# Edge scores of a four-layer graph network: units stationary, one column of signs streamed, scores with slots on partitions

## The chip, the cores and the metric

The kernel runs on one core of one Trainium2 chip. The metric is device time in microseconds (us): the median of several executions of the whole kernel. The engines are PE (TensorE, matrix products; its weight loads are listed apart as PEld), DVE (VectorE), ACT (ScalarE), POOL (GpSimd) and SP (which issues DMAs).

## The reference

Sixteen graphs of 1024 nodes with 128 features go through four layers. Layers 0, 1 and 3 work on the dense 1024x1024 adjacency matrix. The change concerns layer 2 alone, which runs two rounds (`L` = 2) of this:

```python
for l in range(L):
    a = jnp.einsum('bnd,de->bne', x, We1[l, :D])
    b = jnp.einsum('bnd,de->bne', x, We1[l, D:])
    h = jax.nn.relu(a[:, :, None, :] + b[:, None, :, :] + be1[l])
    scores = jax.nn.sigmoid(jnp.squeeze(h @ We2[l], -1) + be2[l])
    upd_adj = adjacency * scores
    messages = jnp.einsum('bnm,bmd->bnd', upd_adj, x)
    ...     # update of x from [x, messages]
```

A pair of nodes with a zero in the adjacency matrix needs no score. About 1.6% of the pairs have an edge, so the kernel before computes the scores of edges only.

## The kernel before

**Buckets and slots.** The 1024 nodes are 8 tiles of 128. A bucket is a pair of tiles (t, u) with t <= u, and holds its edges, undirected, in slots: at most 320 in one of the 28 buckets off the diagonal (`C_OFF`), 480 in one of the 8 diagonal ones (`C_DIAG`). Slots are taken in chunks of 128 (`CK_OFF` = 3, `CK_DIAG` = 4). For each batch `build` makes 0/1 matrices in fp8 for every bucket: `on` and `om` say which node is at either end of a slot (nodes on partitions, slots along the row), and `onT` and `omT` are the same with slots on partitions. `turned` makes such a transposition by matrix products with an identity (tiles `pn`, `pm`). The last chunk of a bucket off the diagonal is half full (`TAIL` = 64); its 64 slots are held twice, in both halves of the partitions, so that the high and the low half of a score can use one product.

**Groups.** Four buckets form a group; a round has seven groups off the diagonal (in which each bucket is done in both directions, so eight rows of scores) and two diagonal ones (four rows). There are 16 x 2 = 32 rounds, hence 224 groups off the diagonal and 64 diagonal ones. For a group:

1. `gather` (L1028): four products bring the parts of both ends to the slots: `pre`, features on partitions, 320 or 480 slots along the row.
2. L1045 (ACT) and L1046 (DVE) apply the relu and split the result in two fp16 halves: `hid`, high and low.
3. `dots` (L1062), as soon as four `hid` are there: the weights We2 were folded into the earlier products with only their signs left, so the score is a sum over features with signs. A 128x32 block of `slide` (zeros but for one column of signs) is stationary, and each half of each `hid` streams through it. The four `hid` write to four 32-partition quarters of one PSUM bank `sc`. Eight products to a call, two calls to a group off the diagonal, one to a diagonal group: 4096 products in the run. A score row lies along the row of one partition.
4. `ends` (L1083, ACT): tanh of the whole `sc` to `srow`. Off the diagonal in two instructions, since the last 64 slots are written twice.
5. `scores`, called while the next group is gathered: transposes of `srow` (L1095, 3 or 4 chunks, fp32) to `pt`, in the same PSUM bank as `sc`; then the columns in use are split in two fp16 halves `u` (L1100 ACT, L1101 DVE, and off the diagonal the small copy L1107); then `val` = `onT` or `omT` times the score (L1120, DVE).
6. `scatter` (L1145): products of `omT`/`onT` with `val` make score matrices `p`; L1153 multiplies by the adjacency; `messages` (L195) multiplies by the features.

**Order.** Every engine works through its own list in order. `weave` mixes three generators by written-down costs: `main` (layer 2 of batch b), `first` (layers 0 and 1 of batch b+1 and its `build`) and `last` (layer 3 of batch b-1). The change leaves these costs alone. PSUM has eight banks: two for `pre`, one each for the lanes `a` and `c`, two for the message sums, one for `sc` (shared with `pt`) and one for `p`.

Of the kernel before, what the change touches and what calls it, by code (L numbers as in the profile page):

```python
# [9 lines left out]
F32 = mybir.dt.float32  # L10
F16 = mybir.dt.float16
FP8 = mybir.dt.float8e4
I32 = mybir.dt.int32
AF = mybir.ActivationFunctionType
OP = mybir.AluOpType
# [36 lines left out]
def tile_four_gnn_layers(  # L52
# [409 lines left out]
    def slots(t, s):  # L462

        return (C_DIAG, CK_DIAG) if t == s else (C_OFF, CK_OFF)

    class Batch:


# [72 lines left out]
    class Edges:  # L541
# [31 lines left out]
        def constants(self):  # L573
            con = self.con
            self.eye16 = con.tile([P, P], F16, name="eye16")
            nc.vector.tensor_copy(self.eye16, ident)
            self.ones16 = con.tile([P, 1], F16, name="ones16")
            nc.vector.memset(self.ones16, 1.0)
            self.iota2 = con.tile([P, HALF], F16, name="iota2")
            self.tri2 = con.tile([P, P], F16, name="tri2")  # L580
            self.low2 = con.tile([P, P], F16, name="low2")
            odd = con.tile([P, CK_DIAG], F32, name="odd")
            i0 = self.a.scratch("i0").bitcast(I32)[:, :Q]
            nc.gpsimd.iota(i0, pattern=[[2, HALF]], base=0, channel_multiplier=0)
            nc.vector.tensor_copy(self.iota2, i0)
            i1 = self.a.scratch("i1").bitcast(I32)[:, 0]
            nc.gpsimd.iota(i1, pattern=[[1, P]], base=0, channel_multiplier=-1)

            nc.vector.tensor_scalar(self.low2, i1, 0.0, 2.0, op0=OP.is_gt, op1=OP.mult)
            nc.vector.tensor_add(self.tri2, self.low2, ident)  # L590
            i2 = self.a.scratch("i2").bitcast(I32)[:, 0, :CK_DIAG]
            nc.gpsimd.iota(i2, pattern=[[2 * P, CK_DIAG]], base=1, channel_multiplier=2)
            nc.vector.tensor_copy(odd, i2)

            iota_off = con.tile([P, CK_OFF * P], F16, name="iota_off")
            nc.vector.tensor_copy(iota_off[:, :C_OFF], self.iota2[:, :C_OFF])
            nc.vector.tensor_copy(iota_off[:, C_OFF:], self.iota2[:, C_OFF - TAIL : C_OFF])
            odd_off = con.tile([P, CK_OFF], F32, name="odd_off")
            nc.vector.tensor_copy(odd_off, odd[:, :CK_OFF])
            last = odd_off[TAIL:, CK_OFF - 1 : CK_OFF]  # L600
            nc.vector.tensor_scalar(last, last, -2.0 * TAIL, None, op0=OP.add)
            self.iota = {True: self.iota2, False: iota_off}
            self.odd = {True: odd, False: odd_off}
            self.c.fine = con.tile([P, 1], F32, name="fine")
            nc.vector.memset(self.c.fine, 1.0)

            self.srow = con.tile([P, CK_DIAG * P], F32, name="srow")
            nc.vector.memset(self.srow, 0.0)

            self.most = con.tile([P, 2], F32, name="most")  # L610
            nc.vector.memset(self.most, 0.0)

        def scaled(self):
# [10 lines left out]
            nc.tensor.matmul(ps, w3T, a3_sb, start=True, stop=True)  # L624
            nc.vector.tensor_copy(v3, ps)
            spread_v3(0)
            self.slide = con.tile([P, L, 2 * G - 1], F16, name="slide16")
            nc.vector.tensor_copy(self.slide, slide)

            self.be2 = con.tile([P, L], F32, name="be2_s")  # L630
            nc.vector.tensor_scalar(self.be2, be2_bc, 0.5, None, op0=OP.mult)
# [193 lines left out]
        def rows_hot(self, s, t, u, name):  # L825

            ck, i = slots(t, u)[1], INDEX[t, u]
            far = self.work.tile([P, HALF], F16, tag="far", name=f"far_{name}")
            nc.scalar.activation(
                far[:, : ck * P], self.iota[t == u][:, : ck * P], AF.Abs, bias=s.mid[:, i : i + 1]  # L830
            )
            on = self.hot_tile("on", t, u, ck * P, name)
            nc.vector.tensor_scalar(
                on, far[:, : ck * P], s.wid[:, i : i + 1], None, op0=OP.is_le, saturate=False
            )
            return on

        def turned(self, hot, ck, name):

            ps = self.a.one(name)  # L840
            for k in range(ck):
                nc.tensor.matmul(  # L842
                    ps[:, k * P : (k + 1) * P], hot[:, k * P : (k + 1) * P], self.eye16,
                    start=True, stop=True,
                )
            return ps

        def build(self, s, has, name):
# [5 lines left out]
            for g, grp in enumerate(GROUPS):  # L854
# [13 lines left out]
                for i, (t, u) in enumerate(grp):  # L868
# [13 lines left out]
                    nc.scalar.activation(onT, pn[:, : ck * P], AF.Copy, saturate=False)  # L882
                    yield 0.35
                    pq = self.a.one(f"pq_{nm}").rearrange("p (k m) -> p k m", m=P)
                    for k in range(ck):
                        nc.tensor.matmul(  # L886
                            pq[:, k], on[:, k * P : (k + 1) * P], rank[:, i], start=True, stop=True
                        )
                    nc.vector.tensor_tensor(  # L889
                        omT.rearrange("p (k m) -> p k m", m=P), pq[:, :ck],  # L890
# [1 line left out]
                        op=OP.is_equal, saturate=False,  # L892
                    )
                    yield 0.35
                    pm = self.turned(omT, ck, f"pm_{nm}")
                    om = self.hot_tile("om", t, u, c, nm)
                    nc.scalar.activation(om, pm[:, :c], AF.Copy, saturate=False)  # L897
                    s.on[t, u], s.om[t, u] = on, om
# [77 lines left out]
        class Group:  # L976
# [3 lines left out]
            def __init__(self, path, s, l, k, msg, name):  # L980
# [3 lines left out]
                self.c, self.ck = slots(*self.grp[0])  # L984
                self.nd = 1 if self.diag else 2
                self.rows = self.nd * Q
                self.per = self.rows // J
                self.hid, self.done, self.sc = [], 0, None

                self.runs = []  # L990
                for i, (t, u) in enumerate(self.grp):
# [60 lines left out]
            def dots(self):  # L1052

                if self.sc is None:
                    self.sc = self.path.bank("sc", f"sc_{self.name}")
                while len(self.hid) - self.done >= J:
                    r = self.done // J

                    order = [(1, J - 1)] + [(0, g) for g in range(J)] + [(1, g) for g in range(J - 1)]
                    with ExitStack() as behind:  # L1060
                        for n, (v, g) in enumerate(order):
                            ins = nc.tensor.matmul(  # L1062
                                self.sc[g * G : (g + 1) * G, : self.c],
                                self.path.slide[:, self.l, G - 1 - r : 2 * G - 1 - r],
                                self.hid[self.done + g][:, v, : self.c],
                                start=(r == 0 and (v, g) in order[: J]),
                                stop=(r == self.per - 1 and (v, g) in order[J:]),
                            )
                            if n == 0:
                                behind.enter_context(tc.issue_after(ins.ins))  # L1070
                    self.done += J

            def ends(self):

                row, once = self.path.srow, self.c if self.diag else self.c - TAIL
                parts = [(row[:, :once], self.sc[:, :once])]
                if not self.diag:
                    parts.append((
                        row[:, once : self.ck * P].rearrange("p (i n) -> p i n", i=2),
                        self.sc[:, None, once : self.c].to_broadcast([P, 2, TAIL]),  # L1080
                    ))
                for dst, src in parts:
                    nc.scalar.activation(  # L1083
                        dst, src, AF.Tanh, bias=self.path.be2[:, self.l : self.l + 1],
                        scale=self.path.down[:, self.l : self.l + 1],
                    )

            def scores(self):


                path, ck, per, name = self.path, self.ck, self.per, self.name
                row = path.srow
                pt = path.bank("sc", f"pt_{name}")
                for k in range(ck):
                    nc.tensor.transpose(pt[:, k * P : (k + 1) * P], row[:, k * P : (k + 1) * P], ident)  # L1095
                pt = pt[:, : ck * P].rearrange("p (c r) -> p c r", r=G)[:, :, :per]
                u = path.work.tile([P, CK_DIAG * J * 2], F32, tag="u", name=f"u_{name}")
                u = u[:, : ck * J * per]
                u2 = u.bitcast(F16).rearrange("p (c r h) -> p c r h", r=per, h=2)
                nc.scalar.activation(u2[:, :, :, 1], pt, AF.Copy, scale=S_SCALE)  # L1100
                nc.vector.scalar_tensor_tensor(  # L1101
                    u2[:, :, :, 0], pt, S_SCALE, u2[:, :, :, 1], op0=OP.mult, op1=OP.subtract
                )
                if not self.diag:

                    again = u2[TAIL:, (ck - 1) * J :]
                    nc.vector.tensor_copy(again[:, :, :, 1], again[:, :, :, 0])  # L1107
                u = u.rearrange("p (k g r) -> p k g r", g=J, r=per)
                self.val, self.ps = {}, [None] * self.nd

                nd = self.nd
                for d in range(nd):
                    for i in range(0, Q, 2):
# [2 lines left out]
                        )  # L1116
                        right = self.s.pairs[self.grp[i]]["omT" if d else "onT"]
                        j = i * nd + d
                        v = u[:, :, j % J : j % J + nd + 1 : nd, j // J : j // J + 1]
                        nc.vector.tensor_tensor(  # L1120
                            pair[:, :, :ck], right, v.rearrange("p k i o -> p i k o").to_broadcast(
                                [P, 2, ck, P]
# [346 lines left out]
```

## Time and profile before

| | |
|---|---|
| median of three runs | 5272.19 us (5258.7 to 5277.03) |
| profiled execution, span | 5272.1 us |
| granted PE clock, mean | 0.986 |
| PE busy | 4924.4 us, 44997 products |
| DVE busy | 4225.4 us |
| ACT busy | 3069.1 us |
| `dots` products (L1062) | 4096, busy 222.2 + 44.4 us |
| transposes of score rows (L1095) | 928, busy 156.2 us |
| tanh of score rows (L1083) | 512, busy 126.1 + 101.7 + 48.0 us |

The span of the profiled execution is the median within 0.1 us, so nothing has to be added around it. Busy time of PE counts a product from its start to its modelled end, and neighbours overlap: three products of 128 columns in a row take 0.33 us, of which only the first 0.055 us each is time that the next can't use. The start of one product to the start of the next is therefore what a product costs.

### The profile page before, as it was taken

How to read it: one execution, taken by the hardware profiler on the slowest of the kernel's cores; microseconds unless marked ns; L12 is line 12 of the kernel's file. 1: busy time of each engine (PE TensorE's matmuls, PEld its weight loads, DVE VectorE, ACT ScalarE, POOL GpSimd, SP SyncE). 2: the span in 40 equal slices, each digit the busy share in tenths (PEclk: the TensorE clock that was granted, in tenths of full speed). 3: DMA queues.
4: the chain of work that ended last, by engine and by line, in shares of the span. 5: the costliest groups of instructions: out<-in, count | busy, mean ns of one | idle time of the engine just before them, and what ended most of it. 6: DMA issues, size and time to landing. Idle time of an engine off the chain costs nothing.

```text
span 5272.1 us, 112168 instructions
## 1 busy us (share of the span) xinstructions
PE 4924.4 (93%) x44997; PEld 3714.9 (70%) x44997; DVE 4225.4 (80%) x9542; ACT 3069.1 (58%) x6790; POOL 199.2 (4%) x137
## 2 busy tenths in 40 slices
PE   6999999999999999999999999999999999999986
PEld 5776777777776777777777776777777777777664
DVE  4776787878879788797887879788797887978876
ACT  5555574665647556575665747556475565756533
POOL 0000000000000000000000000000000000000000
PEclk8999999999999999999999999999999999999998
DMA  6243425243252433424243252432424334242121
GB/s 187 83 127 97 119 59 152 83 132 106 80 155 65 137 98 102 136 66 140 89 123 114 64 165 68 140 100 86 143 75 129 97 102 135 66 139 87 54 64 48
DMA packets 740129, 554.46 MB, mean 105 GB/s; under 512 B 32273, under 2 KB 686353, under 8 KB 739601
## 3 DMA queue, kind: packets, MB, share of 16 engines
q1 hardware_dynamic: 734496, 545.58, 34.8%
q8 instruction: 355, 5.82, 0.5%
q10 hardware_dynamic: 5104, 1.65, 0.1%
q14 instruction: 174, 1.42, 0.1%
HBM read 446.44 MB, written 100.66 MB: 104 GB/s over the span
## 4 chain that ended last, share of the span: by engine, by line
PE 52%; DVE 23%; ACT 13%; DMA 7%; POOL 2%; issue 2%; SPq 0%; ACTq 0%; POOLq 0%; DVEq 0%
PE pre L1028 13%; DVE val L1120 6%; PE p L1145 6%; PE nb L301 6%; PE msg L195 4%; DMA at<-in_adj_dram 4%; PE sc L1062 3%; PE h L355 3%; DVE hid L1046 3%; PE bb L309 3%; PE hp L195 3%; DMA a<-adjT 2%; PE pq L886 2%; ACT hid L1045 2%; PE pn L842 2%
## 5 line engine op out<-in xcount | busy, mean ns | idle before, releaser
L1045 ACT ACTIVATE hid<-pre 128x320 f16<-128x320 f32 (+1 forms) x2048 | 914.6, 453 | 648.3 <-PE pre L1028 597.9
L1046 DVE SCALAR_TENSOR_TENSOR hid<-pre,hid 128x320 f16<-128x320 f32 (+1 forms) x2048 | 1011.8, 506 | 291.3 <-ACT hid L1045 269.6
L1028 PEld LDWEIGHTS <-part 128*128 128x128 f16 x8192 | 749.2, 98 | 410.7 <-issue 179.8
L1028 PE MATMUL pre<-on,part 128*128 128x320 fp8e4 (+1 forms) x4096 | 976.2, 308 | 22.2 <-DVE hid L1046 18.2
L1028 PE MATMUL pre<-om,part 128*128 128x320 fp8e4 (+1 forms) x4096 | 967.0, 308 | 0.0
L195 PE MATMUL msg<-upd,xf 128*128 128x128 f32 (+3 forms) x3008 | 605.4, 321 | 0.7 <-DVE upd L1153 0.6
L1120 DVE TENSOR_TENSOR val<-onT,u 128x768 f32<-128x768 fp8e4 (+1 forms) x576 | 561.1, 1010 | 2.6
L1145 PE MATMUL p<-val,omT 128*128 128x128 f16 x6528 | 498.1, 219 | 50.5 <-DVE val L1120 43.3
L1145 PEld LDWEIGHTS <-omT 128*128 128x128 fp8e4 x6528 | 419.4, 96 | 91.7 <-issue 47.1
L195 PEld LDWEIGHTS msg<-upd,xf 128*128 128x128 f32 x3008 | 418.6, 192 | 20.9 <-DVE upd L1153 2.3
L897 ACT ACTIVATE om<-pm 128x320 fp8e4<-128x320 f32 (+1 forms) x576 | 268.6, 466 | 250.7 <-PE pm L842 247.6
L1120 DVE TENSOR_TENSOR val<-omT,u 128x768 f32<-128x768 fp8e4 x448 | 410.8, 950 | 0.0
L1153 DVE SCALAR_TENSOR_TENSOR upd<-p,adj 128x512 f32<-128x512 f32 x512 | 349.2, 682 | 52.6 <-PE p L1145 48.9
L1145 PE MATMUL p<-val,onT 128*128 128x128 f16 x4480 | 368.2, 219 | 2.4 <-DVE upd L1153 2.4
L195 PE MATMUL hp<-wh,e 128*128 128x129 f32 x2048 | 334.9, 285 | 14.5 <-DVE e L515 14.3
L882 ACT ACTIVATE onT<-pn 128x384 fp8e4<-128x384 f32 (+1 forms) x576 | 297.5, 516 | 83.1 <-PE pn L842 79.3
L1145 PEld LDWEIGHTS <-onT 128*128 128x128 fp8e4 x4480 | 298.6, 97 | 36.1 <-issue 9.9
L1083 ACT ACTIVATE srow<-sc,be_s,down 128x128 f32<-128x128 f32 (+2 forms) x512 | 255.7, 539 | 109.7 <-PE sc L1062 107.8
L195 PEld LDWEIGHTS hp<-wh,e 128*128 128x128 f32 x2048 | 282.1, 195 | 36.4 <-issue 15.0
L301 PE MATMUL nb<-z,l 128*128 128x128 f32 x2048 | 270.8, 282 | 26.2 <-DVE o L342 26.2
L301 PEld LDWEIGHTS nb<-z,l 128*128 128x128 f32 x2048 | 252.9, 196 | 58.5 <-DVE o L342 32.7
L889 DVE TENSOR_TENSOR omT<-pq,odd_off 128x384 fp8e4<-128x384 f32 x448 | 247.5, 552 | 47.3 <-PE pq L886 41.4
(213 smaller groups left out, 8073.3 us busy)
## 6 DMA issues: line engine op xcount, KB each, us to landing
at<-in_adj_dram SPq DMA_DIRECT2D x128, 512.0 KB, 4.0
ct<-in_adj_dram SPq DMA_DIRECT2D x128, 512.0 KB, 4.6
adjT<-tn SPq DMA_DIRECT2D x128, 512.0 KB, 4.8
l<-adjT SPq DMA_DIRECT2D x128, 512.0 KB, 4.4
adj<-adjT SPq DMA_DIRECT2D x256, 256.0 KB, 3.5
a<-adjT SPq DMA_DIRECT2D x128, 384.0 KB, 3.4
adj<-adjT SPq DMA_DIRECT2D x448, 64.0 KB, 2.1
adj<-adjT SPq DMA_DIRECT2D x192, 128.0 KB, 2.6
```

Source lines behind the costliest of these rows:

```text
L195: ins = nc.tensor.matmul(dst, left, right, start=opened is None, stop=True, skip_group_check=True)
L301: nc.tensor.matmul(ps, mat[:, k], z[:, k], start=(k == 0), stop=(k == T - 1))
L882: nc.scalar.activation(onT, pn[:, : ck * P], AF.Copy, saturate=False)
L889: nc.vector.tensor_tensor(omT.rearrange("p (k m) -> p k m", m=P), pq[:, :ck], self.odd[t == u][:, :, None].to_broadcast([P, ck, P]), op=OP ...
L897: nc.scalar.activation(om, pm[:, :c], AF.Copy, saturate=False)
L1028: ins = nc.tensor.matmul(pre[:, :c], path.parts[node // Q][:, k, node % Q, v], hot[:, :c], start=(hot is on and k == 0), stop=(hot is om a ...
L1045: nc.scalar.activation(hid[:, 0, :c], pre[:, :c], AF.Relu)
L1046: nc.vector.scalar_tensor_tensor(hid[:, 1, :c], pre[:, :c], 0.0, hid[:, 0, :c], op0=OP.max, op1=OP.subtract)
L1083: nc.scalar.activation(dst, src, AF.Tanh, bias=self.path.be2[:, self.l : self.l + 1], scale=self.path.down[:, self.l : self.l + 1],)
L1120: nc.vector.tensor_tensor(pair[:, :, :ck], right, v.rearrange("p k i o -> p i k o").to_broadcast([P, 2, ck, P]), op=OP.mult,)
L1145: nc.tensor.matmul(self.ps[d][:, i], left[:, k], halves[:, k, :, h], start=(k, h) == terms[0], stop=(k, h) == terms[-1],)
L1153: nc.vector.scalar_tensor_tensor(upd, self.ps[d], S_SCALE, self.adj[:, d * Q : (d + 1) * Q], op0=OP.add, op1=OP.mult,)
```

## The change

- `dots` swaps its operands. A 128x128 piece of `hid` (128 slots of one half of one row) is stationary, and a single column of signs is streamed. The product writes one column of `sc`: slots on partitions, one column per chunk and row. High and low half add up in the same column. `slide` shrinks to one column of signs per round.
- A piece of 128 slots must be full, so the last chunk starts at slot 192 off the diagonal and at slot 352 on it, and overlaps the one before. `hid_at` and `hot_at` give the starts; `odd`, `odd_off` and `turned_back` are changed to fit, and the diagonal `on` and its far-test take 480 columns instead of 512. `turned_back` streams 64 (diagonal: 96) instead of 128 columns for the last chunk of `pm`.
- `ends` takes tanh of the small `sc` (24 or 16 columns) in one instruction, to a tile `tan` in SBUF.
- The transposes of `srow` and `srow` itself go. `u` is made from `tan`, in the same three instructions as before.
- The first product of a group in the bank is marked as opening it, and the others are issued behind it.

```diff
+    def hot_at(ck):
+        return [k * P for k in range(ck - 1)] + [(C_DIAG if ck == CK_DIAG else CK_OFF * P) - P]
+    def hid_at(ck):
+        return [k * P for k in range(ck - 1)] + [(C_DIAG if ck == CK_DIAG else C_OFF) - P]
...
-            self.slide = con.tile([P, L, 2 * G - 1], F16, name="slide16")
-            nc.vector.tensor_copy(self.slide, slide)
+            self.slide = con.tile([P, L], F16, name="slide16")
+            nc.vector.tensor_copy(self.slide, slide[:, :, G - 1])
...
+        def turned_back(self, hot, c, ck, name):
             ps = self.a.one(name)
             for k in range(ck):
+                lo, hi = k * P, min((k + 1) * P, c)
+                n = hi - lo
+                first = P - n if c == C_DIAG else 0
                 nc.tensor.matmul(
-                    ps[:, k * P : (k + 1) * P], hot[:, k * P : (k + 1) * P], self.eye16,
+                    ps[:, lo:hi], hot[:, k * P : (k + 1) * P], self.eye16[:, first : first + n],
                     start=True, stop=True,
                 )
...
             def dots(self):
...
+                sign = self.path.slide[:, self.l : self.l + 1]
                 while len(self.hid) - self.done >= J:
-                    r = self.done // J
-                    order = [(1, J - 1)] + [(0, g) for g in range(J)] + [(1, g) for g in range(J - 1)]
+                    order = [(J - 1, 1)] + [(g, v) for g in range(J) for v in (1, 0) if (g, v) != (J - 1, 1)]
                     with ExitStack() as behind:
-                        for n, (v, g) in enumerate(order):
-                            ins = nc.tensor.matmul(
-                                self.sc[g * G : (g + 1) * G, : self.c],
-                                self.path.slide[:, self.l, G - 1 - r : 2 * G - 1 - r],
-                                self.hid[self.done + g][:, v, : self.c],
-                                start=(r == 0 and (v, g) in order[: J]),
-                                stop=(r == self.per - 1 and (v, g) in order[J:]),
-                            )
-                            if n == 0:
-                                behind.enter_context(tc.issue_after(ins.ins))
+                        if self.open is not None:
+                            behind.enter_context(tc.issue_after(self.open))
+                        first = None
+                        for g, v in order:
+                            j = self.done + g
+                            for k, at in enumerate(hid_at(self.ck)):
+                                ins = nc.tensor.matmul(
+                                    self.sc[:, k, j : j + 1], self.hid[j][:, v, at : at + P], sign,
+                                    start=self.open is None, stop=True, skip_group_check=True,
+                                ).ins
...
             def ends(self):
-                row, once = self.path.srow, self.c if self.diag else self.c - TAIL
-                parts = [(row[:, :once], self.sc[:, :once])]
-                if not self.diag:
-                    parts.append((
-                        row[:, once : self.ck * P].rearrange("p (i n) -> p i n", i=2),
-                        self.sc[:, None, once : self.c].to_broadcast([P, 2, TAIL]),
-                    ))
-                for dst, src in parts:
-                    nc.scalar.activation(
-                        dst, src, AF.Tanh, ...
+                n = self.ck * self.rows
+                self.tan = self.path.work.tile(
+                    [P, CK_OFF * 2 * Q], F32, tag="tan", name=f"tan_{self.name}"
+                )[:, :n]
+                nc.scalar.activation(
+                    self.tan, self.sc.rearrange("p k j -> p (k j)"), AF.Tanh, ...
             def scores(self):
-                row = path.srow
-                pt = path.bank("sc", f"pt_{name}")
-                for k in range(ck):
-                    nc.tensor.transpose(pt[:, k * P : (k + 1) * P], row[:, k * P : (k + 1) * P], ident)
...
-                nc.scalar.activation(u2[:, :, :, 1], pt, AF.Copy, scale=S_SCALE)
+                nc.scalar.activation(u2[:, :, 1], self.tan, AF.Copy, scale=S_SCALE)
                 nc.vector.scalar_tensor_tensor(
-                    u2[:, :, :, 0], pt, S_SCALE, u2[:, :, :, 1], op0=OP.mult, op1=OP.subtract
+                    u2[:, :, 0], self.tan, S_SCALE, u2[:, :, 1], op0=OP.mult, op1=OP.subtract
                 )
```

## The prediction

> **What bounds the kernel.** First the page's busy row and its chain of work that ended last:
>
> ```profile
> PE 4924.4 (93%) x44997; PEld 3714.9 (70%) x44997; DVE 4225.4 (80%) x9542; ACT 3069.1 (58%) x6790; POOL 199.2 (4%) x137
> ...
> PE 52%; DVE 23%; ACT 13%; DMA 7%; POOL 2%; issue 2%; SPq 0%; ACTq 0%; POOLq 0%; DVEq 0%
> ```
>
> PE is the first limit, DVE the next. Busy PE time contains pipeline tails, so I priced PE by start-to-start times instead and summed them over all products: about 4450 us, 84% of the span. PE holds 52% of the chain, so a microsecond taken from PE is worth between 0.5 and 1. Next, the groups of instructions kept apart by shape, for what the change touches (count | busy us, mean ns | idle before, releaser):
>
> ```profile
> L1062 PE MATMUL sc<-hid,slide 128*32 128x320 f16 x3584 | 222.2, 305 | 10.3 <-DVE hid L1046 8.0
> ...
> L1095 PE MATMUL pt<-ident,srow 128*128 128x128 f32 x928 | 156.2, 278 | 0.2 <-ACT srow L1083 0.2
> ...
> L1083 ACT ACTIVATE srow<-sc,be_s,down 128x256 f32<-128x256 f32 x224 | 126.1, 563 | 78.9 <-PE sc L1062 78.2
> ...
> L1083 ACT ACTIVATE srow<-sc,be_s,down 128x128 f32<-128x128 f32 x224 | 101.7, 454 | 0.0
> ...
> L1083 ACT ACTIVATE srow<-sc,be_s,down 128x480 f32<-128x480 f32 x64 | 48.0, 750 | 30.8 <-PE sc L1062 29.6
> ...
> L800 PE MATMUL pc<-ones,has 128*128 128x1 f16 x576 | 19.1, 163 | 1.2 <-ACT tn L761 1.2
> ```
>
> Row L800 is what makes a price possible: the degree count of `build` already is a product with 128x128 stationary data and one streamed column. Last the timeline (start us, length us), for the true price on PE:
>
> ```profile
> 56.81 0.81 PE L800 MATMUL pc<-ones,has 128*128 128x1 f16 x27 [1.20 <-ACT tn L761]
> ...
> 427.24 0.33 PE L886 MATMUL pq<-rank,on 128*128 128x128 f16 x3
> 427.49 0.59 PE L1062 MATMUL sc<-hid,slide 128*32 128x480 f16 x8
> 428.02 0.45 PE L1028 MATMUL pre<-on,part 128*128 128x320 fp8e4 x2
> ...
> 2003.93 0.50 PE L1095 MATMUL pt<-ident,srow 128*128 128x128 f32 x3
> ...
> 2010.53 0.33 PE L842 MATMUL pn<-eye,on 128*128 128x128 f16 x3
> ...
> 2010.79 0.46 PE L1062 MATMUL sc<-hid,slide 128*32 128x320 f16 x8
> ...
> 2011.17 0.11 PEld L1028 LDWEIGHTS <-part 128*128 128x128 f16 x2 [0.27 <-issue]
> ...
> 2011.18 0.31 PE L1028 MATMUL pre<-om,part 128*128 128x320 fp8e4 x1
> ```
>
> A lone L800 product lasts 0.163 us, so 27 of them in 0.81 start (0.81 - 0.163)/26 = 25 ns apart. Three `pn` use 3 x 55 ns, so PE was free at 2010.695, `sc` began 0.095 later, and the next product came 0.39 after that: a call of `dots` costs 0.485 us. On the diagonal it is 427.405 to 428.02, 0.615 us. Three `pt` last 0.50 and one 0.273, so they start 0.11 us apart.
>
> **What the Trainium skill says.** "TensorE: Matmul & The Clock Gate", section "Wait — 56ns, not 53.3ns?", gives a floor of about 25 ns from start to start however few columns are streamed; L800 shows exactly that here. Its section "Weight-path perf modes — Fast Weight Load (FWL) and DoubleRow" says that a load of 128 columns that isn't fp32 takes a fast path, fp8 more so than 16-bit data. L800 holds fp8, the new stationary data is fp16; the trace has mean loads of 98 ns for fp16 `part` against 96 for fp8 `has`, and two `part` loads in 0.11 us, so 12 to 15 ns apart. I see no fp16 penalty. "TensorEngine Tiling (Array Packing)", section "Key Properties", says that changing the tiling mode drains the engine; the 0.095 us ahead of each `sc` run agrees, and the same again lies behind it (two sets of 320 columns at 0.135 are 0.27 of the 0.39).
>
> **The change part by part.**
>
> *Old products out.* 448 calls x 0.485 = 217 us; 64 x 0.615 = 39 us. The trace shows the calls broken into 591 runs where other work slips between, 79 more than 512, each with a drain at both ends: 79 x 0.19 = 15 us. Together 271 us of PE, the waits for `hid` (10.3 us in the row above) aside, which stay.
>
> *New products in.* A call off the diagonal issues 4 rows x 2 halves x 3 pieces = 24 products, on the diagonal 32: 448 x 24 + 64 x 32 = 12800, at 25 ns 320 us. No mode changes, so no drains, and a broken run costs nothing. PE: +49 us.
>
> *Transposes out.* 928 x 0.11 = 102 us of PE.
>
> *Shorter last piece of `pm`.* 55 ns for 128 columns, so 27 ns less for 64 columns (448 times) and 14 less for 96 (128 times): 14 us of PE.
>
> *Tanh.* From 454 ns at 128 columns and 750 at 480, a column costs 0.84 ns and an instruction 346 ns. The new one costs 346 + 24 x 0.84 = 366 ns, on the diagonal 360. ACT loses 224 x (454 + 563 - 366) + 64 x (750 - 360) = 146 + 25 = 171 us. The diagonal far-test is 32 columns shorter: 3 us more.
>
> *`u`, `val` and the rest.* L1100 stays near 208 ns. L1101 reads SBUF instead of PSUM: 18 ns less by the rows L808 (166 ns) and L809 (184 ns) of like size; x 288 = 5 us of DVE. `val` has the same shapes. No DMA, POOL or SP instruction is touched or moved. Changed constants are a few instructions at the start: under 2 us.
>
> *Waits.* ACT waited 69.5 us for `pt`; that goes, as `tan` is ACT's own. ACT still waits for `sc` (107.8 us before) with the next group's relus queued behind it, and its call is 0.12 us longer now, but its tanh 0.65 shorter. PE's first `dots` of a group no longer waits for DVE to have read `pt` from the bank. One wait moves: the loads used to hold constant signs and ran ahead, now a load is of `hid` itself and waits for DVE. Where PE arrives early this exposes a load, 98 ns. The trace has 26 to 42 such waits of 512, so 4 us; if it came with every call, 512 x 0.098 = 50 us. I take the former, since the drain that it replaces was as long.
>
> *Sum.* PE 49 - 102 - 14 = -67 us, ACT -174, DVE -5. What of it is on the path: summing the pieces of the chain by line, `sc` has 169 us, that is 169/271 = 0.62 of its cost, `pt` 45, `srow` 68, `pm` 64. So 0.62 x 49 = +30; -45; srow 68 x (1 - 94/276) = -45, where 94 and 276 us are the tanh work after and before; `pm` -10. That is -70 us. Counting PE alone gives -34 (0.5) to -67 (1.0). The profiled span is the median, so 5272 - 70 = 5202, say **5200 us**.
>
> **The rivals.**
>
> *A, the forecast:* PE and ACT give up time in about the shares of the chain: 5150 to 5250.
>
> *B, slower: fp16 pieces don't start every 25 ns.* Nothing in the trace has fp16 stationary data with few columns; its place is the run of 24 or 32 pairs in `dots`, with two products into the same column 75 ns apart, which L800 doesn't have either. The bounds are 25 ns and the 55 ns of every 128-column product. The gain is gone when 12800 x d x 0.62 = 70, d = 9, so from 34 ns on. At 40 ns it is 5200 + 12800 x 0.015 x 0.62 = 5320; at 55, 5440. The loads 12 to 15 ns apart speak against it. Exposed loads at every call would add 50 x 0.62 = 31 us and not decide alone.
>
> *C, no change: DVE takes over.* DVE is 80% busy, with blocks such as four `val` in 3.47 us on the chain. If PE and ACT only wait longer for it, the result is DVE's 5 us: 5267. PE's products wait for `val` 43.3 us and for `hid` 35 in all, which is little, and that speaks against it. A changed order of the lists can do as much, in either direction.
>
> *D, more:* ACT's freed blocks let the relus of the next group start earlier, and `pre` banks with them; PE gives its whole 67, ACT's share 45 on top, and half of the 69.5 wait: 5272 - 147 = 5125.
>
> **How the numbers follow.** A has 0.55, D 0.15, C 0.12, B 0.18. Some 0.3% (16 us, so 5256 to 5288) is what a measurement of this kernel can tell from no change. A and D are faster, 0.70; C lies inside, 0.12; B is slower, 0.18. The range starts at 5130, close above D's value of 5125, and so takes in half of D and all of A; it ends at 5275, which takes in most of C. B, from its price of 34 ns on, is left out.
>
> **What would show it.** Right: the new L1062 group with 12800 products, 24 of them in about 24 x 0.025 + 0.14 = 0.74 us of timeline; no `pt` row; tanh near 366 ns; ACT busy near 2895 us; PE without gaps of 0.1 us around `dots`. Wrong: runs of 24 that last over 0.95 us (B); equal PE busy losses but longer PE and ACT waits for `val`, `hid` or `omT` (C).

## The result, and the profile after

The changed kernel takes **5285.48 us** (median of 6 runs, 5277.86 to 5291.36), the kernel before 5267.78 in the same comparison: ratio **1.0033**, 95% interval 1.0021 to 1.0044. It is slower by about 17 us. The prediction was 5200.

The unit prices can be read off at once. First the page of the changed kernel, its busy row and its chain of work that ended last:

```profile
PE 4904.9 (93%) x52773; PEld 3883.7 (73%) x52773; DVE 4207.7 (80%) x9543; ACT 2954.9 (56%) x6566; POOL 176.2 (3%) x137
...
PE 54%; DVE 26%; ACT 9%; DMA 6%; POOL 3%; issue 3%; SPq 0%; ACTq 0%; DVEq 0%; POOLq 0%
```

ACT lost 114 us of busy time and PE 20, and the span grew. Next the groups of instructions by line for the new dots and what follows them (count | busy us, mean ns | idle before, releaser), and the timeline around one call:

```profile
L1091 PE MATMUL sc<-slide,hid 128*128 128x1 f16 x12800 | 399.0, 163 | 11.1 <-DVE hid L1069 8.0
...
L1107 ACT ACTIVATE tan<-sc,be_s,down 128x24 f32<-128x24 f32 (+1 forms) x288 | 106.2, 369 | 122.9 <-PE sc L1091 116.6
...
L1120 ACT ACTIVATE u<-tan 128x24 f16<-128x24 f32 (+1 forms) x288 | 65.8, 228 | 5.7
```

```profile
2000.75 0.30 PE L866 MATMUL pm<-eye,omT 128*128 128x128 f16 x3
...
2000.86 0.68 PEld L1091 LDWEIGHTS <-hid 128*128 128x128 f16 x24
2000.89 0.74 PE L1091 MATMUL sc<-slide,hid 128*128 128x1 f16 x24
...
2001.49 0.43 PE L1051 MATMUL pre<-on,part 128*128 128x320 fp8e4 x2
```

24 products last 0.74 us, (0.74 - 0.163)/23 = 25 ns from start to start, as forecast; no gap of 0.1 us stands before or behind them; there is no `pt` row; tanh takes 369 ns. Of ACT's new instructions only `u` was missed: 228 ns in the mean of its two forms, reading `tan` from SBUF, where it was 204 reading `pt` from PSUM, 7 us in all.

I priced every product of both traces by the least start-to-start time of its form at full clock. That gives 4502 us before and 4437 after, 65 less, where the prediction had 67. So PE did give up its time. The two spans, split by the granted clock (the last row is no further part: it holds the row of what products take longer twice over, and about 13 us of waiting at half clock):

| us | before | after |
|---|---|---|
| products, at full clock | 4502 | 4437 |
| what the same products take longer where the clock is halved | 69 | 119 |
| PE without work to start, at full clock | 687 | 720 |
| all time at half clock | 151 | 250 |

Two things ate the 65 us: 50 us of half clock, and 33 us more of waiting. The waits, first of the kernel before, then of the changed kernel (engine, line, what it waited for: us in total, times, longest):

```profile
  ACT om L897: 5.1, 15
```

```profile
PE pq L910 <- ACT onT L906: 33.8, 70, 0.7
PE pn L853 <- ACT om L921: 32.9, 73, 0.8
PE tp L1214 <- DVE xf L383: 28.1, 30, 1.7
```

(The line of before is from the view of the tile `pn`, of what PE sat idle for ahead of it: us in total, times.) PE arrives at the products that turn one-hot matrices, `pn` and `pq`, before ACT has read the previous bank: 15 such waits for `om` became 73. Also `tp` L1214, the transposes of `xf`, waits for DVE now (1.6 us before).

### The profile page after: what moved, and what is told of

Its sections match the earlier page's. It is cut to its first block, busy times and chain, and to the rows that moved or that the text cites. A ratio compares the mean times of both kernels' runs of the same rounds, so it can differ in the third digit from the quotient of the medians.

```text
span 5289.5 us, 127581 instructions
## 1 busy us (share of the span) xinstructions
PE 4904.9 (93%) x52773; PEld 3883.7 (73%) x52773; DVE 4207.7 (80%) x9543; ACT 2954.9 (56%) x6566; POOL 176.2 (3%) x137
## 4 chain that ended last, share of the span: by engine, by line
PE 54%; DVE 26%; ACT 9%; DMA 6%; POOL 3%; issue 3%; SPq 0%; ACTq 0%; DVEq 0%; POOLq 0%
PE pre L1051 13%; DVE val L1140 7%; PE p L1165 6%; PE nb L301 5%; PE sc L1091 5%; PE msg L195 5%; DVE hid L1069 4%; DMA at<-in_adj_dram 3%; PE bb L309 3%; PE hp L195 3%; PE h L355 3%; PE pq L910 2%; DMA a<-adjT 2%; PE pn L853 2%; DVE omT L913 2%
## 5 line engine op out<-in xcount | busy, mean ns | idle before, releaser
L1051 PE MATMUL pre<-om,part 128*128 128x320 fp8e4 (+1 forms) x4096 | 978.5, 310 | 0.0
L1140 DVE TENSOR_TENSOR val<-onT,u 128x768 f32<-128x768 fp8e4 (+1 forms) x576 | 572.4, 1011 | 3.3
L1091 PEld LDWEIGHTS <-hid 128*128 128x128 f16 x12800 | 378.5, 96 | 64.6 <-DVE hid L1069 44.9
L195 PEld LDWEIGHTS msg<-upd,xf 128*128 128x128 f32 x3008 | 405.5, 191 | 21.9 <-DVE upd L1173 12.1
L1091 PE MATMUL sc<-slide,hid 128*128 128x1 f16 x12800 | 399.0, 163 | 11.1 <-DVE hid L1069 8.0
L195 PE MATMUL hp<-wh,e 128*128 128x129 f32 x2048 | 317.3, 287 | 13.9 <-DVE e L523 13.8
L301 PE MATMUL nb<-z,ct 128*128 128x128 f32 x2048 | 271.0, 285 | 22.7 <-ACT tn L771 20.3
```

The costliest lines, as they stand in the source:

```text
L195: ins = nc.tensor.matmul(dst, left, right, start=opened is None, stop=True, skip_group_check=True)
L301: nc.tensor.matmul(ps, mat[:, k], z[:, k], start=(k == 0), stop=(k == T - 1))
L1051: ins = nc.tensor.matmul(pre[:, :c], path.parts[node // Q][:, k, node % Q, v], hot[:, :c], start=(hot is on and k == 0), stop=(hot is om a ...
L1091: ins = nc.tensor.matmul(self.sc[:, k, j : j + 1], self.hid[j][:, v, at : at + P], sign, start=self.open is None, stop=True, skip_group_ch ...
L1140: nc.vector.tensor_tensor(pair[:, :, :ck], right, v.rearrange("p k i o -> p i k o").to_broadcast([P, 2, ck, P]), op=OP.mult,)
```

## The experiments

In all ratios below the divisor is the kernel before on the same chip. Differences of two ratios are turned into time with 5275 us, and their intervals combine those of the two.

### Is it the clock? The same lists with wider products

After the scheduler has made its lists, the sign column is widened to a sign and zeros, so that each product streams 32, 56 or 120 columns; those behind the first add zero to the columns beside it in the bank. Order and semaphores are those of the changed kernel, but for one memset at the start that writes the zeros. In `w56` the 56 columns are in the program from the start, and the scheduler makes new lists.

```diff
-                                    self.sc[:, k, j : j + 1], self.hid[j][:, v, at : at + P], sign,
+                                    self.sc[:, k * self.rows + j : k * self.rows + j + W], self.hid[j][:, v, at : at + P], sign,
```

> The changed kernel with every list of instructions exactly as it is; only the score products stream 32 columns instead of one, a sign and 31 zeros, so that 31 sums of zero are added to neighbouring columns. At a price of 25 ns from start to start this takes no PE time, but the array streams 13 ns of each 25. Theory clock (the lost gain went to a slower granted PE clock, because runs of one-column products look idle): half-clock time falls from 250 us to under 180, idle and order stay, time 5245 to 5265. Theory order (the lists made for the new durations have worse waits): no change, 5280 to 5290. Theory DVE (PE and ACT freed, DVE binds): no change either, and half-clock time has no effect even if it falls.

> As the run with 32 columns, the lists as they are, but 56 columns streamed (23 ns of each 25). Theory clock: half-clock time back to the 150 us of the kernel before, time 5235 to 5255. Theory order and theory DVE: 5280 to 5290.

> As the run with 56 columns, the lists as they are, but 120 columns streamed: a product should now cost 50 to 53 ns instead of 25, 12800 of them 320 to 350 us of PE more than with 56 columns, with the clock no worse. This measures what a microsecond of PE in the score products is worth. By the share of the chain, 0.62: 200 to 220 us slower than with 56 columns. If PE is not the bound there (theory DVE): less than 80 us.

> The same instructions as the run with 56 columns, but with the lists made anew by the scheduler, which now knows of the 56 columns, so another order on every engine. Theory order: its time differs from that of the 56 columns in the old lists by more than 15 us, in either direction, with PE's waits for ACT and DVE making the difference. Theory clock and theory DVE: equal within 10 us.

| run | start to start | median us | ratio (95%) | time at half clock |
|---|---|---|---|---|
| changed kernel | 25.3 ns | 5285.5 | 1.0033 (1.0021 to 1.0044) | 250 us |
| f32 | 25.3 | 5256.4 | 0.9969 (0.9958 to 0.9981) | 133 |
| f56 | 26.5 | 5268.6 | 0.9988 (0.9981 to 0.9996) | 154 |
| f120 | 53.0 | 5547.1 | 1.0519 (1.0505 to 1.0533) | 110 |
| w56 | 26.5 | 5354.1 | 1.0154 (1.0140 to 1.0168) | 187 |

The groups by line of f32 and f120:

```profile
L1090 PE MATMUL sc<-slide,hid 128*128 128x32 f16 x12800 | 406.6, 177 | 10.8 <-DVE hid L1069 7.4
```

```profile
L1090 PE MATMUL sc<-slide,hid 128*128 128x120 f16 x12800 | 771.6, 217 | 9.3 <-DVE hid L1069 4.9
```

f32 streams 32 times as many columns in the same time of PE, and is 0.0064 of the time, **34 us, faster** than the changed kernel. Nothing but the number of columns differs. The granted clock says why. The trace has only two values of it, 1.0 and 0.5; between 300 and 5180 us each half-clock stretch of the changed kernel lasts 3.41 us or twice that. The table of windows for one drop in the changed kernel (window, length, busy us and count on PE, PEld, DVE, ACT, POOL, then PEclk, DMA share and GB/s), and the timeline of PE in the second of these windows:

```profile
2154.24:2157.65 3.41, 3.41 (x40) 3.19 (x39) 3.41 (x9) 1.93 (x5) 0.00 (x0) 1.00 0.68 193
2157.65:2161.06 3.41, 3.41 (x49) 2.96 (x48) 2.77 (x12) 0.88 (x2) 0.79 (x1) 1.00 0.08 25
2161.06:2164.47 3.41, 3.41 (x18) 2.44 (x19) 0.24 (x2) 2.33 (x7) 0.84 (x1) 0.50 0.00 0
```

```profile
2157.74 0.43 PE L1051 MATMUL pre<-on,part 128*128 128x320 fp8e4 x2
2158.01 0.30 PE L1051 MATMUL pre<-om,part 128*128 128x320 fp8e4 x1
2158.14 0.75 PE L1091 MATMUL sc<-slide,hid 128*128 128x1 f16 x24
2158.76 0.30 PE L1051 MATMUL pre<-om,part 128*128 128x320 fp8e4 x1
2158.89 0.43 PE L1051 MATMUL pre<-on,part 128*128 128x320 fp8e4 x2
2159.16 0.43 PE L1051 MATMUL pre<-om,part 128*128 128x320 fp8e4 x2
2159.43 1.92 PE L391 MATMUL whc_ps<-v,hT 128*128 128x1 f32 x16
```

PE is busy for all 3.41 us of that window, and yet the next is granted half the clock: 40 of its products (`sc` and `whc_ps`) stream one column each, and take over 2 us. The same stretch in f32, where the 24 of `sc` have 32 columns:

```profile
2147.50:2150.91 3.41, 3.41 (x50) 3.04 (x49) 2.69 (x11) 0.87 (x2) 0.88 (x1) 1.00 0.07 24
2150.91:2154.32 3.41, 3.41 (x35) 2.54 (x35) 0.24 (x2) 2.42 (x7) 0.75 (x1) 1.00 0.00 0
```

No drop follows. One stretch could be chance, as the windows of the two runs don't start at the same instruction; over the whole run half clock falls from 250 to 133 us. The Trainium skill ("TensorE: Matmul & The Clock Gate", section "What's actually happening") says that a monitor sets the clock by how busy PE was in free-running windows of 3413 ns, and halves it after an idle one. Stretch and halving are as it says. But in these traces "idle" has to be read as few streamed columns. 320 columns take 135 ns, 0.42 ns each, and 128 fp32 ones 110 ns, so about twice that; with these prices I added up the columns of every such window. All 34 drops of the changed kernel between 300 and 5180 us follow a window with less than 1.34 us of streaming. 36 windows have less than 1.2 us; 10 of them are at half clock already, and 25 of the other 26 are followed by a drop.

f120 against f56 gives the first price of time in the dots: 12800 x 26.5 ns = 339 us more of PE cost 0.0531, 280 us: **0.82 per us**, where 200 to 220 us had been expected. f56 has its half-clock time in the expected place, but at 5269 us is slower than expected: its products start 1.2 ns further apart than those of f32, 15 us of PE, which at 0.82 would be the 12 us between the two. And w56 against f56 has the same products in another order: 86 us apart. So the order of the lists, which every run of the scheduler makes anew, had to be taken out before anything else could be priced.

### The old order with the new products

Here each engine's list is bound to the order of the kernel before, with dependencies that cost no semaphore; the new products stand where the old ones of the same group stood. All streams are 32 columns wide, except in ord1.

```diff
+def in_order(tc, nc, engines):
+    ...     # queue: this engine's instructions in the order of the kernel before
+        for a, b in zip(queue, queue[1:]):
+            tc.add_manual_dep(b, a.name, NoSync, reason="in_order")
...
         path.run()
+        in_order(tc, nc, ("PE", "Activation", "DVE"))
```

`ordact` lets tanh run over 480 columns again (the scores repeated 20 or 30 times), `ordpm` gives the last `pm` product its 128 columns back:

```diff
# ordact
-                self.tan = self.path.work.tile([P, CK_OFF * 2 * Q], F32, ...)[:, :n]
+                tan = self.path.work.tile([P, 480], F32, ..., bufs=1)
+                self.tan = tan[:, :n]
...
-                    self.tan, self.sc[:, :n], AF.Tanh,
+                    tan.rearrange("p (i n) -> p i n", n=n), self.sc[:, None, :n].to_broadcast([P, many, n]), AF.Tanh,
# ordpm
-                    ps[:, lo:hi], hot[...], self.eye16[:, first : first + n],
+                    ps[:, lo : lo + max(n, P - first)], hot[...], self.eye16[:, first : first + max(n, P - first)],
```

> The changed kernel's instructions, with 32 columns streamed by each score product, but PE, ACT and DVE are bound to issue their instructions in exactly the order that they have in the kernel before (score products and tanh in the places of the old ones). Theory order: the loss beside the clock came from the lists made anew. PE needs 66 us less, at the 0.82 us per us that the run with 120 columns gave, so 5273 - 54 = 5219, down to 5190 if ACT's lighter work counts too. Theory DVE (or any loss that belongs to the new way of computing itself): no faster than the 32 columns in the new order, 5245 to 5265.

> As the run in the old order with 32 columns, but one column streamed, so exactly the instructions of the changed kernel in the order of the kernel before. Theory clock: about 29 us slower than with 32 columns in the same order, as in the new order, with the half-clock time 80 to 120 us longer. If clock and order were not separate causes the difference is under 10 us.

> As the run in the old order with 32 columns, but the tanh of each group is taken over 480 columns (the 24 or 16 scores read again and again), so ACT is given back 288 x 0.38 = 110 us of work in the place where the change took it away. By the chain's share for the old tanh (68 of 276 us): 27 us slower. If ACT's lighter work is slack that nobody waits for: under 8 us.

> As the run in the old order with 32 columns, but the last product of each pm off the diagonal streams 128 columns again instead of 64 (448 products, 27 ns more each, 12 us of PE). At 0.82: 10 us slower. If the pm products are never waited for: no difference.

| run | median us | ratio (95%) | against ord32 |
|---|---|---|---|
| ord32 | 5286.0 | 1.0021 (1.0013 to 1.0029) | |
| ord1 | 5292.1 | 1.0029 (1.0018 to 1.0040) | +4 ± 7 us |
| ordact | 5299.3 | 1.0044 (1.0031 to 1.0058) | +12 ± 8 |
| ordpm | 5287.4 | 1.0025 (1.0017 to 1.0033) | +2 ± 6 |

My theory until here, that the scheduler's new order had swallowed the gain, **fell**: with the old order, and with the clock helped, the change is still 11 us slower than before. With 32 columns the new order is even the better one, as f32 is 0.0052, 27 us, below ord32. In the old order one-column products lose little to the clock: ord1 has 177 us at half clock, ord32 162, where the changed kernel has 250 and f32 133. So that loss depends on which products fall into one window. And with one column the two orders take the same time, 1.0029 and 1.0033: the new one has 43 us less of PE without work, and about 70 us more of half clock.

What ordact and ordpm put back is priced far below the chain's share: 110 us of ACT for 12 us, 12 us of PE for 2.

### The transposes, more dots and fewer

`ordpt` puts 928 fp32 transposes (of the identity, result unused) at the old places; `ord64` is ord32 with 64 columns; `ordhalf` leaves out one half of `hid` from the scores, the high one (its expectation, below, says the low one; the number of products is the same, and the dots still wait for DVE's half, 16 us in all in either run); `w32` is f32's program with lists made anew.

```diff
# ordpt
+                pt = path.bank("sc", f"pt_{name}")
+                for k in range(ck):
+                    nc.tensor.transpose(pt[:, k * P : (k + 1) * P], ident, ident)
# ordhalf
-                    order = [(J - 1, 1)] + [(g, v) for g in range(J) for v in (1, 0) if (g, v) != (J - 1, 1)]
+                    order = [(J - 1, 1)] + [(g, v) for g in range(J - 1) for v in (1,)]
```

> The old order of the lists with 32 streamed columns (as in ord32), plus 928 transposes of 32-bit numbers put back on TensorE at the places where the score-row transposes stood; their result is not used by anything. TensorE gets 102 us of work back. If those transposes lay in TensorE's slack (worth 0.13 us per us, as the tanh and the pm products were), the time is about 5299 (+13). If the share of TensorE in the chain of waits prices them (0.44), +45. If TensorE's work counts as in the wide products (0.82), +84.

> As ord32, with 64 streamed columns in place of 32: the score products get 4 to 5 ns longer each, 50 to 58 us of TensorE in all, about the size of what the change added to the dots. If time in the score products lies on the path, 0.82 per us: +41 to +47 us. If small additions are absorbed as the transposes, tanh and pm products are: less than +20.

> As ord32, with only the products of the high halves of hid (6400 instead of 12800); the low halves are left out of the scores. 160 us of TensorE go out of the dots. If time there counts 0.82 per us, -131 us (about 5155). If removals from the dots are absorbed like the others, at 0.1 to 0.2 per us: -16 to -32 us.

> 32 streamed columns in the changed kernel with the lists made anew by the scheduler, in its own order. By the clock alone it equals f32 (0.997 of the kernel before) within 10 us; if the order that the scheduler happens to make is worth as much as between w56 and f56 (86 us), it can be tens of us off either way.

| run | median us | ratio (95%) | PE against ord32 | time against ord32 | per us |
|---|---|---|---|---|---|
| ordpt | 5295.2 | 1.0036 (1.0022 to 1.0049) | +102 us | +8 ± 8 us | 0.08 |
| ord64 | 5326.7 | 1.0094 (1.0078 to 1.0109) | +55 (29.7 ns each) | +39 ± 9 | 0.7 |
| ordhalf | 5206.9 | 0.9860 (0.9845 to 0.9875) | -160 | -85 ± 9 | 0.53 |
| w32 | 5283.6 | 1.0016 (1.0006 to 1.0025) | 0 | -3 ± 7 | |

**102 us of transposes are worth 8 us; 55 us in the dots are worth 39.** Both are work of the same engine in the same list. ordhalf's -85 lies between its two expectations: of a large piece taken from the dots, about half (82 us more of PE without work) is lost to other waits, at `nb`, `pq`, `pm` and others. Where the transposes hide is shown by the groups on PE, of ord32 first and of ordpt below (the last part is the idle time ahead of the group and who ended it):

```profile
L1558 PE MATMUL p<-val,omT 128*128 128x128 f16 x6528 | 498.5, 219 | 58.4 <-DVE val L1533 47.5 <-DVE upd L1566 5.5
...
L1247 PE MATMUL pn<-eye,on 128*128 128x128 f16 x1856 | 197.4, 219 | 32.9 <-ACT om L1315 24.8 <-ACT rank L1284 2.4 <-DVE omT L1307 1.6
```

```profile
L1561 PE MATMUL p<-val,omT 128*128 128x128 f16 x6528 | 498.2, 219 | 47.7 <-DVE val L1536 39.6 <-DVE upd L1569 4.6
...
L1247 PE MATMUL pn<-eye,on 128*128 128x128 f16 x1856 | 197.3, 218 | 17.1 <-ACT om L1315 8.8 <-ACT rank L1284 2.4 <-DVE omT L1307 1.6
...
L1512 PE MATMUL pt<-ident 128*128 128x128 f32 x928 | 153.1, 274 | 0.0
```

With the transposes gone PE waits 24.8 us for `om` ahead of `pn`, with them 8.8 (5.1 before the change); for `val` ahead of `p` 47.5 and 39.6. In my accounting of the traces PE without work at full clock shrinks by 71 us from ord32 to ordpt, in `pn` 21, `p` 16, `pm` 10, `bb` 9, `pre` 8. PE's list is the same in both but for the transposes, so the waits can be compared one by one: counted at either clock they shrink by 84 us, 62 of it within 1 us of the start of a set of transposes. So the transposes stood where PE was about to wait anyway, for work of ACT or DVE that ends as late with or without them. The half clock shrinks too, by 23 us, but that may be chance: executions of ordpt differ between 0.985 and 0.987 in their mean clock, which is 21 us of half clock, and ordall, which has transposes as well, has 160 us of it.

Two things were still open: whether transposes, tanh and `pm` share their slack, so that the three together are worth more than their sum, and whether the removed waits (the transposes for tanh, `u` for the transposes) counted. `ordall` puts all three back linked as they were, and so has little but the dots changed against the kernel before. (Its tanh is one instruction over 480 columns, so 60 of the 170 us of ACT stay away; at ordact's price that is some 7 us, by estimate, by which the dots would cost more than it shows.)

```diff
# on top of ordact and ordpm
+                pt = path.bank("sc", f"pt_{name}")
+                for k in range(ck):
+                    at = min(k * P, 480 - P)
+                    nc.tensor.transpose(pt[:, k * P : (k + 1) * P], self.tan[:, at : at + P], ident)
+                self.tan = pt[:, : ck * self.rows]
```

> As ord32, with all three removed pieces put back together and linked as they were: tanh over 480 columns into one buffer, 3 or 4 transposes of it in the bank of the scores at their old places, u made from what they write, and pm products of 128 columns. The scores reach wrong slots in this one. Against the kernel before it has only the dots changed, so it prices the +49 us of the dots by themselves, and the wait of the transposes for tanh, which ordpt had not. If the prices of ordpt, ordact and ordpm (8 + 13 + 1 us) simply add up, it is at 1.0060 of the kernel before, and the dots cost 32 us (0.65 per us). If the pieces share slack or the removed waits were worth something, it is slower: at the chain shares of the prediction (45 + 45 + 10 us) it would be at 1.021.

5314.4 us, ratio **1.0067** (1.0053 to 1.0081). The sum of the single prices said 1.0060, the chain shares 1.021. The view of the tile `pt` in it shows that the waits are back (what the engine of each line below sat idle for: ACT's `u` for the transposes, DVE's for ACT's `u`, the transposes for `tan`; us, times). The time shows that they cost next to nothing:

```profile
L1513 PE MATMUL pt<-ident,tan x928: 272/273/422, 138.5 to 5225.4; 128*128 128x128 f32 x186
...
  PE pt L1513: 78.2, 78
  ACT u L1518: 14.1, 28
  ACT tan L1500: 4.0, 15
```

So the dots cost 0.0067, 35 us (28 to 43) for 49 us of PE, and the three removals together bring 0.0046, 24 ± 9 us.

Of all kernels run, f32 is the fastest with the full computation: 0.9969 of the kernel before, 16 us. It is the changed kernel with 31 columns of zeros behind the sign and its lists unchanged. w32, the same program with the scheduler's own lists, doesn't keep it.

## Why the prediction was wrong

| step | predicted on the path | found | from |
|---|---|---|---|
| dots, +49 us of PE | +30 | +35 (28 to 43) | ordall against before |
| transposes, -102 us of PE | -45 | -8 ± 8 | ordpt, ord32 |
| tanh, -170 us of ACT | -45 | -12 ± 8, for 110 us of it | ordact, ord32 |
| `pm`, -14 us of PE | -10 | -2 ± 6 | ordpm, ord32 |
| the three together | -100 | -24 ± 9 | ordall, ord32 |
| the scheduler's new order, with 32 columns | 0 (named in C) | -27 ± 7 | f32, ord32 |
| clock, in the new order | 0 | +34 ± 9 | after, f32 |
| sum | -70 | +18 | |

The found column adds up by its making, as it goes from run to run. Its last two steps depend on the way taken: over ord1 the clock is +4 ± 7 (in the old order) and the new order +2 (with one column). That ordall, whose value was forecast from three other runs, landed on 1.0067 for 1.0060 is the test.

**What held.** The durations on PE and that of tanh: 25 ns for the new products, 366 ns for tanh (369), and PE's net 67 us (65 found; all products sum to 4502 us before, not about 4450, which no later step used). The two `u` instructions were missed a little: ACT's didn't stay near 208 ns off the diagonal but takes 230, and DVE's didn't lose 18 ns but went from 180 to 184. Rival B, slower fp16 products, is out. The 4 us for exposed loads can't be told apart from zero. ACT busy is 2955, not 2895, because ACT's records overlap: their summed durations fell by 184 us, tanh by 170 of it, but the time in which two of them overlap fell too, from 416 to 346 us. The two instructions of `srow`, for one, had overlapped by 20 us (255.7 as a group, 275.8 by form).

**What failed, first: "What of it is on the path".** The step that multiplied each removed piece by its share in the chain of waits (45 for `pt`, 45 for `srow`, 10 for `pm`). They measured 8 ± 8, 12 ± 8 and 2 ± 6. The chain is one path, and for a removal its share was no more than a ceiling in these runs: it holds until the next path, of another engine, is as long. For the transposes that was within a microsecond, at `om` and `val`. The bracket that the prediction gave beside it, "from 0.5 to 1.0" for PE's net, had the same fault, and D had it more. For the *added* piece the share was near, 0.62 against 0.72 measured: adding to a chain makes it longer by what is added wherever it has no slack. It isn't the sign alone, though. The prices of the three pieces were measured by putting them back, and half of the dots, taken out in ordhalf, gave 0.53 per us, where the chain of ord32 holds 290 of the dots' 324 us, 0.9. So the share was above what a removal gave each time, but by how much hung on the place: of the transposes' 102 us of PE 84 turn into waits, of the 160 us of dots in ordhalf 82. I used one kind of price for all of them.

**Second: the clock was in no step.** The granted clock before was on record, 0.986, and the change replaced 3584 products of 320 columns and 512 of 480 by 12800 of one. Streamed columns were the one thing that it changed most, and I priced only issue time. In the order that the scheduler made, the clock made the difference to slower: without it (f32) the change would be 0.3% faster. In the old order it wouldn't be, as ord32 shows; there the first fault alone is enough.

**Third: a changed order was named in C, but only as a chance.** It is worth 86 us between w56 and f56, 27 between ord32 and f32, and about as much (25) between f32 and w32: as large as the whole effect. Of the 27 us about half is clock: half clock differs by 31 us between f32 and ord32, and the same products take 16 us less for it. The rest is 13 us less of PE without work, spread over several groups with either sign (`p` -57 us, `pn` +28, `tp` +24); what in the new order makes these isn't settled.

C's sign came true (PE's loss of work turned into waits), but not for its reason: PE's waits for DVE's `val` didn't grow longer, they fell from 43.3 us to 17.0 (before and after):

```profile
L1145 PE MATMUL p<-val,omT 128*128 128x128 f16 x6528 | 498.1, 219 | 50.5 <-DVE val L1120 43.3
```

```profile
L1165 PE MATMUL p<-val,omT 128*128 128x128 f16 x6528 | 501.9, 218 | 21.2 <-DVE val L1140 17.0
```

The new waits are mainly for ACT's evictions of `pn` and `pm` banks, `onT` and `om` above.

## What to carry to other kernels

In these runs a share of the chain of waits came near the price of time added to the dots (0.62 forecast, 0.7 to 0.8 measured); for work taken out it was only a ceiling, and what PE would wait for next has to be looked up at the places where the removed work stands. Before many products with few columns take the place of a few wide ones, look at the granted clock and count streamed columns per window; 31 zeros streamed behind the useful column were free here, as 32 columns start no further apart than one. And where a scheduler makes the lists anew with every edit, compare edits with the order held, or their difference is that of two orders.

## What the runs showed of the hardware that I had not expected

- With 128x128 fp16 stationary data a product takes 25.3 ns from start to start with 1 and with 32 columns, 26.5 with 56, 29.7 with 64, 53.0 with 120. The Trainium skill's floor of about 25 ns ("TensorE: Matmul & The Clock Gate", "Wait — 56ns, not 53.3ns?") holds at 32 columns here and no longer at 56, and with 24 loads in 0.68 us the loads keep up with it.
- A run of one-column products that keeps PE busy without a gap counts as almost nothing for the clock: with the same lists, half clock was 250 us with them and 133 with 32 columns. In the old order the two differ little, 177 and 162 us.
- ACT's copy of 24 columns took 204 ns from PSUM (`u<-pt`, in ordall) and 230 from SBUF (`u<-tan`, in the changed kernel), to the same layout.
